# The causal masks of a four-layer transformer as bfloat16 products of 32 rows and 32 keys, in the row groups of its scores

## The chip, the core and the metric

The kernel runs on one core of a Trainium2 chip. The metric is device time in microseconds for one execution; three executions of the kernel before took 2935.04, 2935.37 and 2937.30 us, median 2935.37. A core has a matrix engine (TensorE, PE in the profile; its loads of the stationary operand are shown apart as PEld), VectorE (DVE), ScalarE (ACT), GpSimd (POOL) and SyncE (SP), which here issues all DMAs. Each engine works through its own instructions in order and waits on semaphores for the others. SBUF is the working memory of 128 partitions; TensorE writes to PSUM, which is handed out here as banks of 128 x 512 float32.

## The reference

The reference applies eight blocks in a row to x of shape (4, 512, 128) in float32, with a residual and a layer norm around each. Here the first and the third matter, and for a small part the fifth and seventh, which are attentions too.

The first block is single-head causal attention with a down-and-up projected value. The third is a transformer of four layers with eight heads of 16 features. Four of the heads look at a window of 128 keys and the 128 before it:

```python
dots = jnp.einsum('bwie,bwje->bwij', bq, bk2) * e ** (-0.5)
mask_value = -jnp.finfo(dots.dtype).max
causal_mask = tix[:, :, :, None] < kix[:, :, None, :]
pad_mask = (kix == -1)[:, :, None, :]
dots = jnp.where(causal_mask | pad_mask, mask_value, dots)
attn = jax.nn.softmax(dots, axis=-1)
```

The other four heads are causal linear attention. Each layer ends with a feed-forward part of width 512.

## The kernel before, in words

The 2048 tokens are cut into eight groups `g` of 512 tokens, each as four tiles of 128 tokens (`NT` = 4). A stage is a set of Python generators, one for each group or each piece of work; `turns` (L392) steps them by a table of start turns, and every `yield` ends a turn. What a generator emits in a turn goes to the engines in exactly that order (a manual schedule). So where an instruction stands in its engine's queue is decided by the turn in which its generator emits it, and a wait in it holds up all that its engine has behind it.

**Loads.** `program` (L1952) issues the loads through `load` (L1965), one DMA on SP for each part of a packed input (L1973). The order on SP is: `x`, small constants and the weights of the first block, the remaining constants, `l1rows`, then the weights of the four transformer layers (L2017), and then what the stages themselves ask for as they are built: after the first stage comes `l1f_quarter` and `phi` of the fourth block.

**First block, `stage_l0` (L563).** `group(g)` (L654) runs attention and feed-forward of one group; a new group starts every four turns. Beside them runs the generator `constants()` (L576): in its first steps it makes the first block's own masks (`negs`, `ident`) on ScalarE, waits eight turns (`idle(8)`, L588), and then converts the three feed-forward weights on VectorE (L590). ScalarE makes for each group the normalised input `xn` (L283), copies of projections out of PSUM (`xT` L596, `wqT`/`wkT` L667, `v` L673), the exponentials `e` (L628) and the transposed weights `eT` (L638).

**Transformer, `stage_l1_attn` (L756).** At its start VectorE and GpSimd fill some buffers (`l_val` L768, `l_max` L770, `l_ctx`), and VectorE casts the identity and the 128 x 128 causal mask to bfloat16 (L773 to L775). Then 32 mixes `l1_mix` (L832; four layers times eight groups) and 32 feed-forwards `l1_ffn` (L810) are interleaved, from the sixth mix on one in eight turns (`at`, L788). PSUM is a ring of seven banks `s`, which also serve as `mm` and `t`, and one bank `o`.

In a mix, all that is of interest is what the two sequences `b` = 0, 1 of the group do for their four local heads. A head's queries and keys lie in 32 partitions, so the four heads are the four row groups of TensorE. For each `b` four banks are taken, one for a head; four products with the identity as the stationary operand write the mask twice (two tiles of diagonal keys, 256 columns) into each bank (L886, through `mm`, L335); then the scores `kT,qT` are added to them, 32 rows each, first of 128 and then of 256 keys. VectorE takes the maxima out of the banks (`l_max`, L894) and joins two of them (L895). Later TensorE transposes the maxima (L908), `q2T` is made of them (L909), and the scores are computed a second time, transposed (`q2T,kT`), for the exponentials `e` on ScalarE (L944), which GpSimd masks (L947) and TensorE multiplies with the values (`e,l_val`). The layer norms run as statistics on VectorE (L255, L257), a power on GpSimd (`ln_rs`, L244 and L245), and normalisation on VectorE (`xn`, L264). GpSimd also adds the biases to the residual `z` (L813, L843).

**Fifth and seventh block.** `attention_pools` (L355) loads two constants, `sel` and `rows`, on SP (`att_sel`, `att_rows`) and casts `rows`, the identity and the mask to bfloat16 on VectorE (L375). Their masks stay as they are. In the seventh block, group 0 squares its rows on ScalarE into a scratch tile `last_sq` to sum them (L1673).

The functions that the change touches, and what calls them:

Of the kernel before, what the change touches and what calls it, by code (L numbers as in the profile page):

```python
# [100 lines left out]
def attention_constants():  # L101


    p = np.arange(P) % 32
    c = Pack()
    c.add("sel", ((p[:, None] < 12) & (p[:, None] % 4 == np.arange(4)[None, :])).astype(np.float32))
    c.add("rows", np.tile((p[:, None] < 12).astype(np.float32), (1, P)))
    return c


def packs(i):

    out = {"const": constants(), "att": attention_constants()}
    a = out["l0"] = Pack()
    a.add("wq", i["L0_attn_Wq"])
    a.add("wk", i["L0_attn_Wk"])
    a = out["l0v"] = Pack()
    a.add("down", i["L0_attn_Wvdown"].T)
    a.add("up", i["L0_attn_Wvup"])
    a = out["l0f"] = Pack()  # L120
    a.add("gate", i["L0_ffn_w_gate"].T)
    a.add("up", i["L0_ffn_w_up"].T)
    a.add("down", rows_to_partitions(i["L0_ffn_w_down"].T))
    r = out["l1rows"] = Pack()
    for k in range(4):
        a = out[f"l1_{k}"] = Pack()
        wq, wk, wv = (i[f"L1_attn_W{x}"][k] for x in "qkv")
        a.add("wq", heads_padded(wq[:, :64]))
        a.add("wk", heads_padded(wk[:, :64]))
        a.add("tok", np.concatenate([wq[:, 64:], wk[:, 64:], wv], axis=1))  # L130
        a.add("wo", i["L1_attn_Wo"][k])
        a.add("w1", i["L1_attn_W1"][k])
        a.add("w2", rows_to_partitions(i["L1_attn_W2"][k]))
        a.add("b1", i["L1_attn_b1"][k].reshape(4, P).T)
        for x in ("ln1_g", "ln1_b", "ln2_g", "ln2_b"):
            a.add(x, i[f"L1_attn_{x}"][k][:, None])
        r.add(f"bo{k}", i["L1_attn_bo"][k][None])
        r.add(f"b2{k}", i["L1_attn_b2"][k][None])
    a = out["l1f"] = Pack()
    a.add("phi", i["L1_ffn_phi"])  # L140

    p = np.arange(P)
    a.add("quarter", ((p[:, None] % 32 == np.arange(P)[None, :] // 32) & (p[:, None] < 96)).astype(np.float32))
    a = out["l1fb"] = Pack()
    a.add("b", i["L1_ffn_b"].reshape(16, 4, D).transpose(1, 0, 2))
    a = out["l1fw"] = Pack()
    a.add("w", i["L1_ffn_W"].transpose(1, 0, 2))
    a = out["l2"] = Pack()
    for x in "qkvo":
        a.add("w" + x, i["L2_attn_W" + x])  # L150
    a.add("w1", i["L2_ffn_w1"])
    a.add("w2", rows_to_partitions(i["L2_ffn_w2"]))
    a.add("b1", i["L2_ffn_b1"].reshape(4, P).T)
    r.add("l2b2", i["L2_ffn_b2"][None])
    a = out["l3"] = Pack()
    p = "L3_attn_"
    a.add("in", i[p + "in_proj_w"])
    for x in "BC":
        a.add(x, i[p + x + "_proj_w"].reshape(D, 16, 64)[:, SCAN_HEADS])
    a.add("out", rows_to_partitions(i[p + "out_proj_w"]))  # L160
    a.add("mfc", i[p + "m_fc_w"])
    a.add("mproj", rows_to_partitions(i[p + "m_proj_w"]))
    kw = np.repeat(i[p + "k_w"].reshape(D, 4, 1, 8), 4, axis=2).reshape(D, 128)
    a.add("qkv", np.concatenate([i[p + "q_w"], kw, i[p + "v_w"]], axis=1))
    a.add("o", i[p + "o_w"])
    a.add("afc", i[p + "a_fc_w"])
    a.add("aproj", rows_to_partitions(i[p + "a_proj_w"]))
    a.add("convw", rows_to_partitions(i[p + "conv_w"]))
    a.add("convb", i[p + "conv_b"].reshape(2, P).T)
    a.add("gain", np.repeat(i[p + "q_gain"], 8)[:, None])  # L170
    a.add("D", np.repeat(i[p + "D_param"], 16).reshape(2, P).T)
    a = out["l3rows"] = Pack()
    for x in ("resid_mix_m", "resid_mix_a"):
        a.add(x, i[p + x].reshape(1, -1))
    for x in ("mamba_scale", "m_mlp_scale", "attn_scale", "a_mlp_scale", "dt_bias", "A_log"):
        a.add(x, i[p + x][None])
    a = out["moe"] = Pack()
    a.add("gate", i["L3_ffn_gate_w"])
    for e in range(8):
        a.add(f"w1_{e}", i["L3_ffn_w1"][e])  # L180
        a.add(f"w2_{e}", rows_to_partitions(i["L3_ffn_w2"][e]))
    return out
# [17 lines left out]
class Ctx:  # L200
# [154 lines left out]
    def attention_pools(self):  # L355

        nc = self.nc
        self.vm = [self.t([P, NT, 4, D], f"at_vm{i}", 1) for i in range(2)]  # L360
        self.pieces = [self.t([P, 2, 4, 32], f"at_pc{i}", 1, dt=BF16) for i in range(2)]
        for a in self.vm + self.pieces:
            nc.gpsimd.memset(a, 0.0)
        for a in self.vm:
            for v in range(4):
                at = a[:, :, v, :].rearrange("p t (r n) -> p t r n", r=4)
                lo = 16 * (v % 2) + 8
                nc.gpsimd.memset(at[:, :, :, lo : lo + 8], 1.0)
        self.cb = {n: self.t([P, P], "b_" + n, 1, dt=BF16) for n in ("ident", "negmask", "rows")}
        self.sel = self.t([P, 4], "at_sel", 1)  # L370
        with self.tc.tile_pool(name="att", bufs=1) as pool:
            got = self.load(pool, "att")
            nc.vector.tensor_copy(self.sel, got["sel"])
            for n, a in (("ident", self.c["ident"]), ("negmask", self.c["negmask"]), ("rows", got["rows"])):
                nc.vector.tensor_copy(self.cb[n], a)  # L375

    def variants(self, src, tag):

        nc, mask = self.nc, self.c["head8"]
        out = self.t([P, 4, GT], tag, 2)  # L380
        for v in (0, 1):
            nc.scalar.activation(out[:, v, :], src, AF.Copy, scale=mask[:, v : v + 1])
        nc.gpsimd.tensor_tensor(out[:, 2:4, :], bc(src, 1, 2), bc(mask[:, 2:4], 2, GT), ALU.mult)
        return out

    def values_put(self, g, v, src):

# [175 lines left out]
def stage_l0(k, x, w, wv, wi, z, l1, y7, xT0):  # L563
# [12 lines left out]
    def constants():  # L576
        full = k.t([P, P], "negs", 1)
        gp.memset(full, NEG)
        gp.memset(negs[:, 2, :], 0.0)
        yield  # L580
        nc.scalar.copy(negs[:, 1, :], full)
        nc.scalar.copy(ident, k.c["ident"])
        ps = k.ps("s")
        k.mm(ps[:, :D], wv["down"], wv["up"])
        nc.scalar.copy(wfull, ps[:, :D])
        for t in (0, 3):
            nc.scalar.copy(negs[:, t, :], k.c["negmask"])
        yield from idle(8)  # L588
        for name in f:
            v.tensor_scalar(f[name], wi[name], float(np.float32(1.0 / 127.0)), None, ALU.mult)  # L590
            yield
# [164 lines left out]
def stage_l1_attn(k, x, ws, rows, z, then, xn, y7, xT0):  # L756
# [13 lines left out]
        nc.gpsimd.memset(a, 0.0)  # L770
    for a in k.l1_ctx:
        nc.gpsimd.tensor_copy(a[:, :, 64:68], bc(k.c["head16"], 1, 4))
    k.cb = {n: k.t([P, P], "b_" + n, 1, dt=BF16) for n in ("ident", "negmask")}  # L773
    for n, a in k.cb.items():
        nc.vector.tensor_copy(a, k.c[n])  # L775

    def ffn(i, g):
        late = i == 3 and g in k.over
# [53 lines left out]
def l1_mix(k, z, w, bo, n, hT=None):  # L832
# [1 line left out]


    nc, v = k.nc, k.nc.vector
    ident, negmask = k.cb["ident"], k.cb["negmask"]
    val, lin, ctx, mx = k.l1_val[n % 3], k.l1_lin[n % 3], k.l1_ctx[n % 2], k.l1_max[n % 2]
    heads = [slice(32 * h, 32 * h + 32) for h in range(4)]
    tiles = lambda b: [slice((2 * b + t) * P, (2 * b + t + 1) * P) for t in range(2)]  # L840
# [40 lines left out]
    for b in range(2):  # L881
        (q0, q1), both = tiles(b), slice(2 * b * P, (2 * b + 2) * P)
        ss = [k.ps("s") for _ in heads]


        for s in ss:  # L886
            k.mm(s[:, : 3 * P].rearrange("p (j n) -> p j n", j=3)[:, 0:3:2, :], ident, bc(negmask, 1, 2), True, False)
        for r, s in zip(heads, ss, strict=True):
            k.mm(s[:, 0:P], qT[r, q0], kT[r, q0], False, False)
        for r, s in zip(heads, ss, strict=True):  # L890
            k.mm(s[:, P : 3 * P], qT[r, q1], kT[r, both], False, True)
        for h, s in enumerate(ss):
            s = s[:, : 3 * P].rearrange("p (j n) -> p j n", j=3)
            v.tensor_reduce(mx[:, b, :, h, 16], s, AX.X, ALU.max, negate=True)  # L894
        v.tensor_tensor(mx[:, b, 1, :, 16], mx[:, b, 1, :, 16], mx[:, b, 2, :, 16], ALU.min)  # L895
        if b == 0:
            yield
            yield
# [729 lines left out]
def l3_gqa(k, x, xa, w, gain, mix, first):  # L1628
# [31 lines left out]
    def tail(g, yT):  # L1660
# [7 lines left out]
        if g == 0:  # L1668

            ss = k.t([P, NT], "last_ss", 1)  # L1670
            sq = k.t([P, D], "last_sq", 1)
            for t in range(NT):
                nc.scalar.activation(sq, xa[g][:, t, :], AF.Square, accum_out=ss[:, t : t + 1])  # L1673
            yield
            k.rsqrt(k.kept[0], ss, 1.0 / D, RMS_EPS)

# [275 lines left out]
def program(ctx: ExitStack, tc: tile.TileContext, xin, dram, at, out):  # L1952
# [42 lines left out]
    const.update(load(base, "const", set(at["const"]) - {"ident", "negmask"}))  # L1995
    k = Ctx(tc, const, None, None)
    k.load = load
    k.mhalf = base.tile([P, P], F32, tag="mhalf", name="mhalf")
    nc.gpsimd.memset(k.mhalf, -0.5)
    k.over = {g: base.tile([P, NT], F32, tag=f"over{g}", name=f"over{g}") for g in (NG - 2, NG - 1)}  # L2000
# [88 lines left out]
```

## Time and profile before

| what | value |
|---|---|
| median of three executions | 2935.37 us (2935.04 to 2937.30) |
| span of the profiled execution | 2932.0 us (3.4 us under that median) |
| TensorE busy (PE) | 2732.5 us, 93% |
| loads of stationary operands (PEld) | 1849.0 us, 63% |
| VectorE, ScalarE, GpSimd busy | 1951.7, 1713.0, 1017.2 us |
| mean granted TensorE clock | 0.967 |
| the first block | to about 173 us |
| the transformer | about 174 to 910 us; 21 steady periods of 22.49 us from 362 us on, then four of about 24 us |

The profile is one execution of the program on the chip. A line of a group or timeline names the source line, the engine, the operation, what it writes and reads (tile names without buffer numbers), the shape, and how often; for a matmul the shape begins with rows*columns of the array that it uses. In a timeline the first number is the start and the second the duration of the merged stretch, both in microseconds. Brackets give the idle time of the engine before the stretch and what ended it. A float32 product stands as two records, one for each pass. `b_negmask,b_ident` are the mask products. Ends of matmuls are modelled and overlap, so distances between starts say more than durations. In the chain of waits, each piece was released by the one before it.

### The profile page before, as it was taken

The numbers are of one execution on the slowest core, as the hardware profiler recorded it, in microseconds if no ns is written. First come the engines' busy times: TensorE is split into PE (matmuls) and PEld (weight loads), VectorE is DVE, ScalarE is ACT, GpSimd is POOL, SyncE is SP. The second block draws the span as 40 slices with busy tenths as digits, with TensorE's granted clock in tenths as the row PEclk, the third lists the DMA queues.
The fourth block names the chain that finished last, engine by engine and source line by source line (L and its number), as shares of the span: only waits on it lengthen the run. The fifth ranks groups of instructions, "written<-read, shape, count | busy, mean of one in ns | idle before, by whom it ended". The sixth has DMA issues, their size and how long they took to land.

```text
span 2932.0 us, 59643 instructions
## 1 busy us (share of the span) xinstructions
PE 2732.5 (93%) x23674; PEld 1849.0 (63%) x23674; DVE 1951.7 (67%) x5309; ACT 1713.0 (58%) x3568; POOL 1017.2 (35%) x1406
## 2 busy tenths in 40 slices
PE   8989999999998699999978997999999799988998
PEld 5656667766666588888843443566666444436897
DVE  5765666666676999999776774666574686737442
ACT  6746566666665577777635665444444377756443
POOL 3543333333345100000054554422231466645332
PEclk9999999999999799999989998899999899999999
DMA  4000000000000000000010000000000000010000
GB/s 105 12 1 1 2 1 2 2 2 2 5 12 27 6 14 11 10 11 9 18 62 5 1 2 1 1 1 1 1 1 1 2 1 1 1 39 21 1 16 16
DMA packets 30158, 31.30 MB, mean 11 GB/s; under 512 B 7404, under 2 KB 21292, under 8 KB 29868
## 3 DMA queue, kind: packets, MB, share of 16 engines
q1 hardware_dynamic: 29880, 27.49, 3.2%
q8 instruction: 187, 3.06, 0.4%
q14 instruction: 91, 0.75, 0.1%
HBM read 23.29 MB, written 4.19 MB: 9 GB/s over the span
## 4 chain that ended last, share of the span: by engine, by line
PE 67%; DVE 10%; ACT 9%; POOL 4%; issue 2%; DMA 0%; SPq 0%; POOLq 0%; ACTq 0%; DVEq 0%
PE ps_s L336 41%; PE ps_o L336 11%; PE ps_mm L336 7%; PE ps_s L325 3%; ACT e L944 2%; ACT at_e L491 1%; POOL ln_rs L245 1%; PE ps_t L1218 1%; DVE xn L264 1%; PE ps_xin L336 1%; PE ps_sum L336 1%; ACT L944 1%; POOL e L947 1%; DVE l_max L894 1%; ACT lg L1213 1%
## 5 line engine op out<-in xcount | busy, mean ns | idle before, releaser
L459 DVE TENSOR_REDUCE at_nm<-ps_s 128x2 f32<-128x512 f32 (+1 forms) x384 | 238.1, 681 | 118.9 <-PE ps_s L336 118.9
L491 ACT ACTIVATE at_e<-ps_s 128x512 f32<-128x512 f32 x384 | 198.1, 604 | 96.2 <-PE ps_s L336 94.0
L1502 DVE TENSOR_TENSOR scan<-ps_s,lm 128x384 f32<-128x384 f32 x256 | 124.6, 548 | 142.4 <-PE ps_s L336 142.2
L497 POOL TENSOR_SCALAR_AFFINE_SELECT at_e<-at_e 128x1024 f32<-128x1024 f32 (+1 forms) x96 | 135.1, 1407 | 209.2 <-ACT at_e L491 208.9
L245 POOL TENSOR_TENSOR ln_rs<-ln_rs,mhalf 128x4 f32<-128x4 f32 x192 | 196.3, 1022 | 15.7
L1026 POOL TENSOR_TENSOR ln_rs<-ln_mv,mendt 128x4 f32<-128x4 f32 x6 | 1.2, 198 | 510.6 <-DVE mend L1247 507.1
L244 POOL TENSOR_SCALAR ln_rs<-ln_mv 128x4 f32<-128x4 f32 x184 | 39.6, 215 | 372.9 <-DVE ln_mv L257 357.5
L894 DVE TENSOR_REDUCE l_max<-ps_s 128x3 f32<-128x384 f32 x256 | 124.8, 551 | 53.6 <-PE ps_s L336 51.2
L336 PE MATMUL ps_o<-my,meT 128*128 128x129 f32 x1024 | 142.2, 284 | 15.3 <-ACT mgot L1232 7.9
L947 POOL TENSOR_SCALAR_AFFINE_SELECT e<-e 128x512 f32<-128x512 f32 x128 | 78.9, 637 | 218.5 <-ACT e L944 218.5
L336 PE MATMUL ps_s<-qm,kT 32*128 32x512 f32 x768 | 144.3, 654 | 8.0 <-DVE at_nm L459 7.8
L336 PEld LDWEIGHTS ps_o<-my,meT 128*128 128x128 f32 x1024 | 125.8, 192 | 38.1 <-ACT meT L1220 24.4
L336 PE MATMUL ps_s<-km,qT 32*128 32x512 f32 x768 | 137.8, 664 | 11.6 <-DVE qT L1646 3.7
L336 PE MATMUL ps_mm<-mdisp,mxn 128*128 128x128 f32 x1024 | 129.5, 284 | 10.5 <-DVE mdisp L1134 10.5
L336 PEld LDWEIGHTS ps_o<-l_w,mlp_h 128*128 128x128 f32 x1024 | 126.1, 192 | 19.1 <-issue 12.8
L336 PE MATMUL ps_o<-at_e,at_vm 128*32 128x128 f32 (+1 forms) x2048 | 123.1, 337 | 15.3 <-ACT at_oT L521 15.3
L336 PE MATMUL ps_s<-mphi,mxT 128*128 128x256 f32 x448 | 123.2, 395 | 14.2 <-DVE mpart L1095 13.9
L336 PE MATMUL ps_s<-b_negmask,b_ident 128*128 128x256 bf16 (+1 forms) x640 | 125.6, 306 | 9.8 <-DVE b_negmask L775 3.1
L336 PE MATMUL ps_o<-l_w,mlp_h 128*128 128x128 f32 x1024 | 130.4, 276 | 4.0 <-ACT oT L964 3.9
L336 PEld LDWEIGHTS ps_mm<-mdisp,mxn 128*128 128x128 f32 x1024 | 124.6, 200 | 14.0 <-DVE mdisp L1134 11.9
L1479 ACT COPY BT<-ps_s 128x512 f32<-128x512 f32 x64 | 37.5, 587 | 158.1 <-PE ps_s L336 158.1
L336 PEld LDWEIGHTS <-b_ident 128*128 128x128 bf16 x656 | 57.6, 100 | 108.9 <-issue 89.1
(470 smaller groups left out, 7272.1 us busy)
## 6 DMA issues: line engine op xcount, KB each, us to landing
mw<-in_l1fw SPq DMA_DIRECT2D x16, 256.0 KB, 2.6
moe_w<-in_moe SPq DMA_DIRECT2D x16, 256.0 KB, 5.5
l_w<-in_l SPq DMA_DIRECT2D x10, 256.0 KB, 3.6
x<-in_x SPq DMA_DIRECT2D x8, 256.0 KB, 4.4
xs<-x SPq DMA_DIRECT2D x8, 256.0 KB, 2.2
out<-x SPq DMA_DIRECT2D x8, 256.0 KB, 2.3
slT<-xs SPq DMA_DIRECT2D x6, 256.0 KB, 2.7
mphi<-in_l1f SPq DMA_DIRECT2D x7, 128.0 KB, 2.0
```

The costliest lines, as they stand in the source:

```text
L244: g.tensor_scalar(out, in_, scale, eps, ALU.mult, ALU.add)
L245: g.tensor_tensor(out, out, self.mhalf[:, :n], ALU.pow)
L325: self.nc.tensor.transpose(out[:n, k * P : (k + 1) * P], src[:, k, cols], self.c["ident"])
L336: self.nc.tensor.matmul(out, lhsT=lhsT, rhs=rhs, start=start, stop=stop, skip_group_check=True)
L459: v_.tensor_reduce(nm[:, t, r, vs], s, AX.X, ALU.max, negate=True)
L491: nc.scalar.activation(e[:, r], s, AF.Exp)
L497: nc.gpsimd.affine_select(at, at, [[0, 4], [0, n], [1, P]], ALU.is_ge, 0.0, base=0, channel_multiplier=-1)
L894: v.tensor_reduce(mx[:, b, :, h, 16], s, AX.X, ALU.max, negate=True)
L944: nc.scalar.activation(e[:, h].rearrange("p j n -> p (j n)"), s[:, : 3 * P], AF.Exp)
L947: nc.gpsimd.affine_select(e[:, :, j, :], e[:, :, j, :], [[0, 4], [1, P]], ALU.is_ge, 0.0, base=0, channel_multiplier=-1)
L1479: nc.scalar.copy(s, ps)
L1502: v.tensor_tensor(m, s[:, : SEQ + P], lm[:, SCAN_HEADS[4 * (t // 2) + 2 * i + hh], :], ALU.mult)
```

## The change

- A new packed input `masks` of two parts is loaded in the first block by `constants()`: `tri` (128 x 512 float32, 256 KB) and `one` (128 x 32, 16 KB). After the eight idle turns ScalarE casts both to bfloat16 into tiles that live for the whole program (`k.tri`, `k.one`).
- The 128 x 128 mask is written in four pieces `c` of 32 keys. For each piece and each head, a 32 x 128 block of `tri` is the stationary operand, in the row group of that head, and `one` (a 32 x 32 identity, read twice) streams 64 columns. So a group of four products of 256 columns becomes sixteen products of 64 columns, each with its own load, in the order: piece 0 for the four banks, piece 1 for the four banks, and so on. The scores follow as before.
- The casts of identity and mask at the start of the transformer (L773 to L775) go.
- `rows` is loaded as one column (0.5 KB instead of 64 KB), and the cast reads it as a broadcast.
- The squares of group 0 in the seventh block are written into the tile `y`, which is free by then, instead of `last_sq`.

```diff
-    c.add("rows", np.tile((p[:, None] < 12).astype(np.float32), (1, P)))
+    c.add("rows", (p[:, None] < 12).astype(np.float32))
...
+def mask_constants():
+    p = np.arange(P)
+    c = Pack()
+    behind = 32 * np.arange(4)[None, :, None] + (p % 32)[:, None, None] > p[None, None, :]
+    c.add("tri", np.where(behind, NEG, 0.0).astype(np.float32))
+    c.add("one", (p[:, None] % 32 == np.arange(32)[None, :]).astype(np.float32))
+    return c
...
-            for n, a in (("ident", self.c["ident"]), ("negmask", self.c["negmask"]), ("rows", got["rows"])):
+            for n, a in (("ident", self.c["ident"]), ("negmask", self.c["negmask"]), ("rows", got["rows"].to_broadcast([P, P]))):
...
+    def masked(self, banks):
+        tri = self.tri.rearrange("p (c q) -> p c q", c=4)
+        for c in range(4):
+            for r, s in enumerate(banks):
+                k = slice(32 * r, 32 * r + 32)
+                self.mm(s[:, :, 32 * c : 32 * c + 32], tri[k, c, :], bc(self.one[k], 1, s.shape[1]), c == 0, False)
...
             nc.scalar.copy(negs[:, t, :], k.c["negmask"])
+        got = k.load(k.work, "masks")
         yield from idle(8)
+        for to, name in ((k.tri, "tri"), (k.one, "one")):
+            nc.scalar.copy(to, got[name])
         for name in f:
...
-    k.cb = {n: k.t([P, P], "b_" + n, 1, dt=BF16) for n in ("ident", "negmask")}
-    for n, a in k.cb.items():
-        nc.vector.tensor_copy(a, k.c[n])
...
-        for s in ss:
-            k.mm(s[:, : 3 * P].rearrange("p (j n) -> p j n", j=3)[:, 0:3:2, :], ident, bc(negmask, 1, 2), True, False)
+        k.masked([s[:, : 3 * P].rearrange("p (j n) -> p j n", j=3)[:, 0:3:2, :] for s in ss])
...
-            sq = k.t([P, D], "last_sq", 1)
             for t in range(NT):
-                nc.scalar.activation(sq, xa[g][:, t, :], AF.Square, accum_out=ss[:, t : t + 1])
+                nc.scalar.activation(y[:, t, :], xa[g][:, t, :], AF.Square, accum_out=ss[:, t : t + 1])
...
+    k.tri, k.one = (base.tile([P, at["masks"][n][1]], BF16, tag="mask_" + n, name="mask_" + n) for n in ("tri", "one"))
```

More of the change, by code (lines that the diff above doesn't have):

```diff
@@ L106, in attention_constants @@
     c.add("sel", ((p[:, None] < 12) & (p[:, None] % 4 == np.arange(4)[None, :])).astype(np.float32))
-    c.add("rows", np.tile((p[:, None] < 12).astype(np.float32), (1, P)))
+    c.add("rows", (p[:, None] < 12).astype(np.float32))
[6 more added lines that the diff above has]
+    c.add("one", (p[:, None] % 32 == np.arange(32)[None, :]).astype(np.float32))
     return c
 def packs(i):
-    out = {"const": constants(), "att": attention_constants()}
+    out = {"const": constants(), "att": attention_constants(), "masks": mask_constants()}
     a = out["l0"] = Pack()
@@ L836, in l1_mix @@
     nc, v = k.nc, k.nc.vector
-    ident, negmask = k.cb["ident"], k.cb["negmask"]
     val, lin, ctx, mx = k.l1_val[n % 3], k.l1_lin[n % 3], k.l1_ctx[n % 2], k.l1_max[n % 2]
```

## The prediction

> **What bounds the kernel now.** I read the page's span and chain first, then the chain of waits and the timeline of one steady period of the four-layer transformer (where the masks are), then the timeline of ScalarE and of the SP queue at the start of the run (where the new load and its casts fall).
>
> The page: its span, its chain by engine, and the group of all mask products.
>
> ```profile
> span 2932.0 us, 59643 instructions
> PE 67%; DVE 10%; ACT 9%; POOL 4%; issue 2%; DMA 0%; SPq 0%; POOLq 0%; ACTq 0%; DVEq 0%
> L336 PE MATMUL ps_s<-b_negmask,b_ident 128*128 128x256 bf16 (+1 forms) x640 | 125.6, 306 | 9.8 <-DVE b_negmask L775 3.1
> ```
>
> Two thirds of the chain is TensorE. Of the 640 mask products 256 (64 groups of four) are the transformer's; the rest belong to two other attentions and stay.
>
> The timeline of ScalarE, then of the SP queue, in the first stage (start, duration), and the time to landing of the DMAs issued from 37 to 42 us.
>
> ```profile
> 24.62 0.58 ACT L638 COPY eT<-ps_s 128x512 f32<-128x512 f32 x1 [0.95 <-PE ps_s L636]
> 26.98 0.58 ACT L673 COPY v<-ps_s 128x512 f32<-128x512 f32 x1 [1.77 <-PE ps_s L336]
> 27.46 1.65 ACT L283 ACTIVATE xn<-x,ln_nb,ln_rs 128x128 f32<-128x128 f32 x4
> ```
> ```profile
> 41.25 0.43 SPq L1973 DMA_DIRECT2D l1f_quarter<-in_l1f  x1
> 41.72 0.43 SPq L2030 DMA_DIRECT2D phi<-in_l1f  x1
> ```
> ```profile
> l_w<-in_l SPq DMA_DIRECT2D x2, 256.0 KB, 3.3
> phi<-in_l1f SPq DMA_DIRECT2D x1, 128.0 KB, 2.3
> l1f_quarter<-in_l1f SPq DMA_DIRECT2D x1, 64.0 KB, 1.9
> ```
>
> The queue issues one load each 0.47 us, and the loads behind the transformer's weights go out only at 41.25 us. By then ScalarE has long passed 25 us.
>
> The windows: span, then busy time of PE, PEld, DVE, ACT, POOL. The first follows the `v` copy above; the second is one steady period.
>
> ```profile
> 26.98:60.00 33.02, 31.64 (x158) 18.85 (x157) 23.53 (x121) 25.75 (x64) 12.78 (x24) 1.00 0.32 75
> 433.88:456.37 22.49, 22.25 (x220) 15.70 (x219) 14.23 (x52) 14.28 (x31) 7.84 (x11) 1.00 0.01 2
> ```
>
> Both are dense on TensorE, so time lost in the first stage is not made good from slack, and the steady period looks as if any saving on TensorE would count. The next views say it does not. The chain of waits of a steady period where its first mask group (A) stands, then VectorE, GpSimd and TensorE up to the transposes of the maxima:
>
> ```profile
> 474.88 0.79 ACT e L944 x2
> 475.66 0.04 issue
> 475.70 1.14 PE ps_s L336 x17
> ```
> ```profile
> 476.86 1.95 DVE L894 TENSOR_REDUCE l_max<-ps_s 128x3 f32<-128x384 f32 x4 [1.27 <-PE ps_s L336]
> 478.93 0.86 DVE L255 BATCH_NORM_STATS2 ln_st<-z 128x6 f32<-128x128 f32 x4
> 482.17 0.54 DVE L895 TENSOR_TENSOR l_max<-l_max 128x4 f32<-128x4 f32 x1
> ```
> ```profile
> 481.41 1.27 POOL L813 TENSOR_TENSOR z<-z,l1rows 128x512 f32<-128x512 f32 x1
> ```
> ```profile
> 478.70 0.60 PE L336 MATMUL ps_s<-b_negmask,b_ident 128*128 128x256 bf16 x4
> 479.23 0.94 PE L336 MATMUL ps_s<-kT,qT 32*128 32x128 f32 x16
> 482.32 0.78 PE L908 MATMUL ps_s<-const_ident,l_max 128*128 128x128 f32 x4
> ```
>
> The last mask of group A waits until 475.70 for a bank that an exponential frees. From the scores behind it VectorE works without a gap (maxima, L895, statistics, aggregates, to 480.07), which releases GpSimd's `ln_rs` and then its sum L813 (to 482.69). L895 of group B, 0.17 us long elsewhere, lasts 0.54 and ends at 482.71, right after L813; the fourth transpose of the maxima waits for it. Group B (478.70) lies inside that path, not on it.
>
> **The change part by part.** The sum is made against the profiled execution (span 2932.0); the median of the three runs is 2935.4, so 3.4 us lie around the span, and I keep them.
>
> *The load of the masks and its casts (first stage): the large term.* The generator issues the load at its second step, but SP works in order, and the built SP order has `masks_tri` (256 KB) and `masks_one` (16 KB) right behind the last transformer weight, where `l1f_quarter` is now: issue 41.25 and 41.72. Landing: quarter and phi together, 192 KB, are in by 41.72 + 2.3 = 44.0; 64 KB more at the pace at which phi followed quarter (128 KB in 0.85 us) gives 44.4. The two casts stand on ScalarE between the `eT` copy, which ends at 25.2, and the `v` copy. So ScalarE stands still from 25.2 to 44.4 us. Then 0.5 us for the 128x512 cast (the like copies start 0.48 apart) and 0.2 for the small one: `v` starts at about 45.2, not 26.98: +18.2. With the 256 KB load at 2.6 us (the sixteen `mw` loads) or 3.9 (the slowest `l_w` from 30 us on) it is 17.5 to 18.9. Queued behind: every later ScalarE instruction; TensorE first misses the `xn` of 27.46 (its transposes at 29.04), and after it VectorE and GpSimd. Given back: what waited for VectorE is ready by then (ScalarE idled 0.69 us before `e` at 31.25): -0.7, from 0 to -1.5. Added: TensorE is idle for 17 us. After the idle stretch that ends at 134.76 its clock was granted at 0.55 until 137.0 and 0.78 from there to 140; about 3.6 us at half speed is 1.8 us of work, some of it beside ScalarE: +1.2, from 0 to 2.5. Sum for this stage **+18.7**, bounds +16.0 and +21.4. The loads behind move by 0.95 us and are wanted hundreds of us later: nothing.
>
> *The masks, 256 products of 256 columns to 1024 of 64.* Now: a group's products start 0.109 us apart ((0.60 - 0.273)/3); from its first to the scores' first load is 0.53, of which 0.09 is the pause that TensorE shows at each switch of row groups. After it, the pause comes ahead of the masks and none behind. What a 32-row bfloat16 product costs is not in a mask row; the nearest row is the one of four 32-row bfloat16 products:
>
> ```profile
> 1568.20 0.39 PE L336 MATMUL ps_s<-at_mT,b_rows 32*128 32x512 bf16 x4
> ```
>
> Alone each lasts 0.374, so four groups start within 0.02: 7 ns apart, side by side. A product of 64 columns streams 0.027 (256 take 0.107). A round of four so costs 0.027 (7 ns each) to 0.054 (load and stream in turn); the far bound is 0.107, the step of the 128-column float32 scores. A group: 0.09 + 0.2 = about 0.28 instead of 0.53, a quarter of a microsecond less, 16 us over 64 groups if all of it counted.
>
> It does not. Steady periods (21 of 22.49 us): group A's last bank comes at 475.70 whatever TensorE does; from there to the scores is 0.20 now, and three rounds, 0.08 to 0.16, afterwards: 0.07 saved. Group B's saving ends in the wait for L895, which moves with group A alone. 21 x 0.07 = **-1.5**, from -2.4 to +2.7 (rounds of 0.107).
>
> [...] The row shows 7 ns between row groups, so I go by the row.
>
> The first eight mixes, with long waits on other engines and TensorE at clock 0.50 (178 to 187 us): groups take up to 1.0 us there; half of 16 groups x 0.25: **-2.0**, from 0 to -6. The last four periods (24.05 us, no bank wait): 4 x 0.18 = **-0.7**, from 0 to -1.5.
>
> *The two casts of L775 gone.* 0.2 us on VectorE at 176.2, counted in the -2.0: TensorE's 3.1 us wait for them gives nothing more, as kT is ready only at 174.9 and VectorE is late anyway with statistics, `qm` and maxima.
>
> *`rows` as one column.* The DMA of 64 KB becomes 0.5 KB. VectorE waited 0.37 us for it at 1518.2, once: **-0.3** (0 to -0.4); the second is not waited for. *Squares into `y`*: four activations of 0.31, same engine and size: 0, hidden by the 2.4 us that ScalarE waits ahead of them; without that cover a write wait, under 0.1.
>
> Sum: +18.7 - 1.5 - 2.0 - 0.7 - 0.3 = **+14.2**, 2935.4 + 14.2 = 2949.6.
>
> **The rivals.**
> 1. *TensorE's saving counts in full.* For it: TensorE is busy 22.25 of 22.49 us. Against: the wait of the fourth transpose for L895. It would give 18.7 - 16 - 0.3 = +2.4, 2938.
> 2. *The stall is absorbed* (the other side): the landing comes before ScalarE needs it, or the casts cost nothing because the stage has 18 us to spare. For it: only that ScalarE is busy 25.75 of 33.02 us. Against: issue at 41.25, and TensorE at 31.64 of 33.02. It gives -4.5, 2930.9; it decides if `masks_tri` lands before about 27 us.
> 3. *Both at once*: -16.3, 2919.
> [...]
>
> **How the numbers follow.** Forecast 0.80; rival 1 0.08, rival 2 0.03, rival 3 0.03, rival 4 0.06. The forecast's bounds add to +5.7 (16.0 - 2.4 - 6 - 1.5 - 0.4) and +24.1, ends that need every term at its edge; I take 2940 to 2957, which leaves out rivals 2 and 3, half of 1 and half of 4. A measurement tells 0.2% (5.9 us) from no change: slower (above 2941.3) 0.89, within 0.2% 0.07, faster 0.04.
>
> **What the profile after would show.** ScalarE idle from 25.2 to about 44.4 us in front of the cast of `mask_tri`, released by a DMA; the first stage longer by 16 to 21 us (`l_val` memsets at about 192.5, not 173.9); mask groups of sixteen that take 0.1 to 0.25 us, without a pause before the scores; the steady period between 22.35 and 22.49 us; TensorE waiting longer ahead of L908. The prediction is wrong if the casts are released early, or if the period falls to about 22.0.

## The result, and the profile after

The changed kernel takes 2944.7 us (median of five, 2942.39 to 2952.05), the kernel before 2935.04 us beside it: ratio 1.0036 with a 95% interval of 1.0025 to 1.0047, so 7 to 14 us slower. The profiled execution has a span of 2940.7 us, 8.7 more than that of before.

The page of the kernel after, its span and its chain by engine:

```profile
span 2940.7 us, 61176 instructions
PE 65%; DVE 15%; ACT 11%; POOL 5%; issue 2%; SPq 1%; DMA 1%; POOLq 0%; ACTq 0%; DVEq 0%
```

VectorE's share of the chain has grown from 10 to 15%; where it came in is seen below. First the loss. The timeline of ScalarE of the kernel after in the first stage (start, duration, in brackets the idle time ahead and what ended it), then the SP queue and the time to landing:

```profile
25.88 0.58 ACT L662 COPY eT<-ps_s 128x512 f32<-128x512 f32 x1 [1.20 <-PE ps_s L660]
42.67 0.62 ACT L612 CAST mask_tri<-masks_tri 128x512 bf16<-128x512 f32 x1 [16.21 <-DMA masks_tri<-in_masks]
43.20 0.21 ACT L612 CAST mask_one<-masks_one 128x32 bf16<-128x32 f32 x1
43.32 0.58 ACT L697 COPY v<-ps_s 128x512 f32<-128x512 f32 x1
```
```profile
39.91 0.43 SPq L1991 DMA_DIRECT2D masks_tri<-in_masks  x1
```
```profile
masks_tri<-in_masks SPq DMA_DIRECT2D x1, 256.0 KB, 2.7
```

ScalarE stands still for 16.21 us until the DMA lands, and the `v` copy comes at 43.32 instead of 26.98. The windows after the `v` copy and of one steady period answer to those shown of before (span, busy time of PE, PEld, DVE, ACT, POOL, granted clock):

```profile
43.32:76.34 33.02, 31.15 (x143) 17.84 (x144) 16.36 (x75) 25.48 (x64) 7.09 (x13) 0.92 0.01 2
462.37:484.75 22.38, 21.72 (x243) 15.28 (x243) 14.35 (x51) 14.29 (x31) 7.84 (x11) 1.00 0.00 1
```

TensorE is 0.53 us less busy in a steady period (22.25 before), but the period is only 0.11 shorter. If each instruction is set against the same one of before, its delay is +16.6 us at 60 us; +15.1 at the end of the first stage (`l_val` memsets at 189.0, before 173.9); +9.5 when the steady periods begin; +6.9 at 900 us. After that only code that is nearly the same follows, and yet there are steps of +1.7 (at 922), -3.0 (at 1520 to 1565), +4.5 (2610 to 2640) and -1.5 (2725 to 2900), to +8.5 at the end. The runs below separate most of these pieces.

### The profile page after: what moved, and what is told of

Its sections match the earlier page's. It is cut to its first block, busy times and chain, and to the rows that moved or that the text cites. A ratio compares the mean times of both kernels' runs of the same rounds, so it can differ in the third digit from the quotient of the medians.

```text
span 2940.7 us, 61176 instructions
## 1 busy us (share of the span) xinstructions
PE 2717.4 (92%) x24442; PEld 1834.2 (62%) x24442; DVE 1953.8 (66%) x5307; ACT 1712.8 (58%) x3570; POOL 1018.4 (35%) x1406
## 4 chain that ended last, share of the span: by engine, by line
PE 65%; DVE 15%; ACT 11%; POOL 5%; issue 2%; SPq 1%; DMA 1%; POOLq 0%; ACTq 0%; DVEq 0%
PE ps_s L347 40%; PE ps_o L347 10%; PE ps_mm L347 7%; DVE l_max L913 3%; PE ps_s L336 2%; ACT e L963 2%; POOL ln_rs L256 1%; ACT at_e L512 1%; DVE ln_st L266 1%; DVE xn L275 1%; PE ps_t L1237 1%; PE ps_xin L347 1%; POOL e L966 1%; PE ps_sum L347 1%; ACT L963 1%
## 5 line engine op out<-in xcount | busy, mean ns | idle before, releaser
L347 PE MATMUL ps_s<-xT,l_w 128*128 128x512 f32 x256 | 126.1, 613 | 2.5 <-ACT xT L827 1.3
L275 DVE TENSOR_SCALAR xn<-z,ln_mv,ln_rs 128x128 f32<-128x128 f32 x252 | 74.9, 361 | 70.1 <-POOL ln_rs L256 70.1
```

The costliest lines, as they stand in the source:

```text
L275: self.nc.vector.tensor_scalar(out[:, k, :], src[:, k, :], mv[:, k, 0:1], rs[:, k : k + 1], ALU.subtract, ALU.mult)
L347: self.nc.tensor.matmul(out, lhsT=lhsT, rhs=rhs, start=start, stop=stop, skip_group_check=True)
```

## The experiments

All ratios are against the kernel before on the same chip, with their 95% interval.

### Only the load and its casts

The kernel before with the change's load and casts, where the change has them; its own masks are used as before, and the cast ones by nobody.

```diff
             nc.scalar.copy(negs[:, t, :], k.c["negmask"])
+        got = k.load(k.work, "masks")
         yield from idle(8)
+        for to, name in ((k.tri, "tri"), (k.one, "one")):
+            nc.scalar.copy(to, got[name])
```

> The kernel before with the change's load and casts, at the same places, and nothing else of it; all masks are written as before and the cast masks are not used. Theory: +15.1 to +16.6 us from the first stage, 2950 to 2952 us (ratio 1.0050 to 1.0058), and no other step in the trace beyond what two executions differ by; the transformer's periods stay at 22.49 us. The change stands at +9.7, so the masks' own saving would be 5.5 to 7. Rival (the late stages' steps of +1.7, -3.0 and +4.5 us in the change's trace belong to the load or the first stage's shift): they appear here too, with the same signs and places. Rival (absorbed): 2935.

Measured: 2950.45 us, ratio 1.0048 (1.0035 to 1.0061), 10 to 18 us slower. ScalarE waits 15.81 us for `masks_tri` and casts at 42.55; the delay is +16.6 us at 60 us and +15.1 at the end of the stage, as in the change; the steady periods stay at 22.49. So the load and its casts are the loss, and in the traces the rest of the change is a gain of 5.4 us by 900 us (+12.3 here, +6.9 with the change). Of the change's late steps, that at 922 us and that of +4.5 at 2610 to 2640 us do not appear here, and 1520 to 1565 us brings +3.3 instead of -3.0: the load does not make them.

It also shows that the profile of before is not a clean yardstick. With unchanged masks, this kernel gains 1.6 us at 225 to 260 us and 1.4 at 335 to 362 us. The windows of these stretches, first of the kernel before, then of this one (the third number from the right is the granted TensorE clock):

```profile
225.00:260.00 35.00, 32.73 (x298) 22.77 (x297) 19.61 (x60) 21.27 (x49) 10.74 (x15) 0.95 0.00 1
335.00:362.00 27.00, 25.48 (x239) 17.75 (x238) 15.22 (x57) 14.61 (x34) 8.78 (x12) 0.94 0.00 1
```
```profile
225.00:260.00 35.00, 32.63 (x325) 21.36 (x325) 26.13 (x88) 20.19 (x48) 13.07 (x19) 1.00 0.00 1
335.00:362.00 27.00, 25.16 (x264) 17.89 (x263) 18.25 (x63) 14.71 (x33) 7.85 (x11) 1.00 0.01 2
```

In the profiled execution of before, TensorE's clock was granted at half speed for a moment in each of them (0.50 from 230.49 to 233.90 and from 339.72 to 343.13 us); here it was not. The drop from +16.6 to +15.1 at about 135 us, in both kernels with the stall, lies where before had a clock of 0.61 (134 to 138 us); at its counterpart in the changed kernel (150 to 154 us) it is 1.00. This one is no accident of one profile: each of the ten executions without the stall has such a stretch between 112 and 159 us, and neither of the two with the stall has. The other two come and go: the kernel before with GpSimd's sum moved (below) has the first and not the second, the one with late casts the second and not the first.

### Late casts, and an early load

Two ways to take the wait away and keep the masks. The first moves the casts nine turns back:

```diff
-        for to, name in ((k.tri, "tri"), (k.one, "one")):
-            nc.scalar.copy(to, got[name])
         for name in f:
             v.tensor_scalar(f[name], wi[name], float(np.float32(1.0 / 127.0)), None, ALU.mult)
             yield
+        yield from idle(6)
+        for to, name in ((k.tri, "tri"), (k.one, "one")):
+            nc.scalar.copy(to, got[name])
```

> Only the place of the two mask casts on ScalarE differs from the change: they are emitted nine turns later, long after the masks have landed (42.7 us). Theory (the first stage's stall is the whole loss): ScalarE no longer stands still from 26.5 us on, the l_val memsets come at 174 to 175 us (before 173.9, after 189.0), and the time falls by 15.1 to 16.6 us against the change: 2928 to 2930 us, about 6 us under the kernel before (ratio 0.997 to 0.999). Rival (the stage absorbs the stall, or the loss lies in the later stages): the memsets come earlier but the time stays at 2942 to 2946. Second rival (the casts themselves cost ScalarE): 0.7 us are kept, not told apart here.

The second leaves the casts and issues the load ahead of the transformer's rows and weights:

```diff
+    k.masks = load(p0, "masks")
     rows1 = load_rows(base, "l1rows")
...
-        got = k.load(k.work, "masks")
+        got = k.masks
```

> The casts stand where the change has them, but the masks are loaded ahead of the transformer's rows and weights, issued at about 17.8 us instead of 39.91. Theory (what ScalarE waits for is the place of the load in SP's queue): landing at 20.5 to 22 us, before ScalarE comes to the casts at 26.5, no stall, and the same time as with late casts, 2928 to 2931 us; the casts then cost 0.7 us on ScalarE at most. Rival (the casts at that place are what costs, by their order on ScalarE ahead of the v copy): most of the stall stays, 2940 us or more.

Measured: 2927.86 us, ratio 0.9974 (0.9963 to 0.9984), and 2928.4 us, 0.9975 (0.9966 to 0.9983): both 5 to 11 us faster than before. The `l_val` memsets come at 173.7 us with late casts, where they were before. With the early load, issued at 17.24, ScalarE of that kernel goes straight from the `eT` copy into the casts, and then still waits for TensorE ahead of the `v` copy, which hides them:

```profile
28.02 0.58 ACT L662 COPY eT<-ps_s 128x512 f32<-128x512 f32 x1 [0.95 <-PE ps_s L660]
28.50 0.62 ACT L612 CAST mask_tri<-masks_tri 128x512 bf16<-128x512 f32 x1
29.02 0.22 ACT L612 CAST mask_one<-masks_one 128x32 bf16<-128x32 f32 x1
30.38 0.58 ACT L697 COPY v<-ps_s 128x512 f32<-128x512 f32 x1 [1.14 <-PE ps_s L347]
```

So neither the place of the casts on ScalarE nor the casts themselves cost anything measurable; the lateness of the load at that place does. This execution is 3.4 us late by 28 us, not because of the early load: the first run of the moved sum below, whose load is not early, is 3.7 us late there too. What makes them late is not shown.

### New masks in one group alone

Late casts, and the new products only for one of the two sequences, the old ones for the other; the casts of identity and mask on VectorE are back.

```diff
-        k.masked([s[:, : 3 * P].rearrange("p (j n) -> p j n", j=3)[:, 0:3:2, :] for s in ss])
+        if b == 0:
+            k.masked([s[:, : 3 * P].rearrange("p (j n) -> p j n", j=3)[:, 0:3:2, :] for s in ss])
+        else:
+            for s in ss:
+                k.mm(s[:, : 3 * P].rearrange("p (j n) -> p j n", j=3)[:, 0:3:2, :], k.cb["ident"], bc(k.cb["negmask"], 1, 2), True, False)
```

The other kernel has `b == 1` in the condition.

> Late casts; the new mask products only for the first sequence (group A), the old four products of 256 columns for the second (group B), with the casts of identity and mask on VectorE back. Theory (group A is on the period's path, group B's saving ends in the wait for VectorE): the steady periods fall as with all new masks, by 0.11 us each (stretch from 400 to 800 us shorter by 1.9 to 2.0), and the transformer as a whole keeps at least 3 of the 7 us. Rival (every group's TensorE time counts): half, 0.05 to 0.06 us a period, 1.0 in that stretch.

> Late casts; the new mask products only for the second sequence (group B). Theory: the steady periods stay at those of before, within 0.02 us (0 to 0.3 in the stretch from 400 to 800 us), although group B's masks take 0.13 instead of 0.53 us, and TensorE's fourth transpose of the maxima waits longer for VectorE's join; some of the first eight mixes may gain. Rival (every group's TensorE time counts): 0.05 to 0.06 us a period, as for group A. If both kernels gain and their sum is that of all new masks, the rival stands.

Measured: 2931.93 us, ratio 0.9992 (0.9983 to 1.0000), and 2931.98 us, 0.9992 (0.9983 to 1.0001). The times can't tell them apart; the traces can, one execution each (distances between VectorE's joins of group A's maxima; of the first six distances the sum):

| masks | first six mixes, us | steady period, us | last periods, us | group B's join, us |
|---|---|---|---|---|
| old in both (load and casts alone) | 135.26 | 22.49 | 24.04 | 0.53 |
| new in A | 134.42 | 22.37 | 23.91 | 0.49 |
| new in B | 133.38 | 22.49 | 24.03 | 0.76 |
| new in both (late casts) | 132.72 | 22.375 | 23.92 | 0.77 |

In the steady periods the whole gain of 0.115 us is group A's; group B's products give nothing, and the join after them lasts 0.23 us longer. In the first six mixes, where no join is held (0.17 us each), group B gives 1.9 us and A 0.8 by the table; but the first of these distances varies by itself (15.34 to 16.01 us in seven executions with all new masks). In the other five B gives 0.9 us, A 0.5 and both together 1.3. The rival of equal shares falls.

### What holds group B

The join L895 (L914 in the changed kernel) ends right after GpSimd's bias sum in every steady period. The first try emitted that sum one turn later:

```diff
-    k.nc.gpsimd.tensor_tensor(z, z, bc(b2, 1, NT), ALU.add)
     yield
     h = k.t([P, 4, GT], "mlp_h", 2)
...
+        if f == 1:
+            k.nc.gpsimd.tensor_tensor(z, z, bc(b2, 1, NT), ALU.add)
         if f % 2:
             yield
```

> Late casts as in the run of that name, and GpSimd's sum of the bias into z in the feed-forward is emitted one turn later, so that it no longer lies beside VectorE's join of the maxima. Theory (group B's saving ends in the wait for that join, which lasts until GpSimd's sum ends, 0.54 to 1.09 us instead of 0.17): the join falls to about 0.17 us, TensorE's fourth transpose of the maxima comes 0.3 to 0.6 us earlier, and a period falls from 22.38 to between 21.8 and 22.2 us: 5 to 15 us under the run with late casts alone. Rival (another wait takes its place, the bank that an exponential frees or VectorE's own work): the join shortens, the period stays within 0.1 us of 22.38, and the time within 3 us of the run with late casts. Second rival (the sum at its new place delays GpSimd's masking of e or ln_rs, or holds another operation of VectorE): slower by some us.

Measured: 2929.56 us, ratio 0.9980 (0.9969 to 0.9990), steady period 22.38, join 0.76. The edit moved nothing: GpSimd has no other instruction in that turn, so the sum still followed `ln_rs` at once. Nothing follows from it but that a later place in the code is not a later time. The second try puts it behind GpSimd's next two instructions, `l_ctx` and the mix's bias sum, with the new masks and late casts, and alone in the kernel before:

```diff
     ps = k.ps("o").rearrange("p (t d) -> p t d", t=NT)
+    k.nc.gpsimd.tensor_tensor(z, z, bc(b2, 1, NT), ALU.add)
     w2 = w["w2"].rearrange("p (c n) -> p c n", c=4)
```

> Late casts, and GpSimd's sum of the feed-forward's bias is emitted two turns later, behind the product for l_ctx and the mix's own bias sum in GpSimd's queue (one turn later, in the run before, moved nothing: GpSimd had nothing in between and started it at the same place). Theory (VectorE's join of group B is held until that sum ends): the join falls from 0.77 to 0.17 us in every period, the 0.26 us that TensorE waits ahead of the fourth transpose go, a period falls by 0.2 to 0.35 us, and the time by 5 to 10 us against late casts alone: 2918 to 2923 us. Rival (VectorE's own chain or a bank takes over): the join shortens, the period stays within 0.05 us. Rival (the join's length is its own, whatever GpSimd does): it stays at 0.77 us.

> The kernel before with the same move of GpSimd's sum and nothing else. If group B's saving only waits behind the held join, this gains less than the same move does with the new masks, by up to 0.2 us a period. If VectorE's own work between the two groups' maxima (join of A, statistics, maxima of B) hides group B's masks anyway, both gain the same: what the old join loses, 0.54 minus 0.17 us less what TensorE is late by itself, 0 to 0.2 us a period, 0 to 6 us in all (2929 to 2937).

Measured: with the new masks 2921.49 us, ratio 0.9955 (0.9943 to 0.9967); alone 2930.9 us, 0.9989 (0.9979 to 0.9998). All joins fall to 0.17 us, in the kernel before too. With the new masks the period falls by 0.475 us against late casts, more than the 0.2 to 0.35 expected, and 0.3 us more than the same move gives alone (expected: up to 0.2 more). The steady periods make a table of two by two:

| steady period, us | sum where it was | sum two turns later |
|---|---|---|
| old masks | 22.49 | 22.32 |
| new masks | 22.375 | 21.90 |

With the join held the masks save 0.115 us a period, without it 0.42. So group B's saving was there and ended in the wait for the held join: that rival (VectorE's own chain hides it) falls. The chain of waits over one period from group A's last bank to the transposes of the maxima shows how, first of the kernel before, then of the change, then of the change with late casts and the later sum (start, duration, engine, tile, line):

```profile
453.21 1.14 PE ps_s L336 x17
454.35 1.44 PE ps_o L336 x32
455.78 0.59 PE ps_s L325 x4
456.37 3.62 PE ps_s L336 x40
459.99 0.61 PE ps_s L908 x4
```
```profile
462.37 1.06 PE ps_s L347 x29
463.43 1.95 DVE l_max L913 x4
465.39 0.17 DVE l_max L914
465.56 0.78 DVE ln_st L266 x4
466.34 0.28 DVE ln_mv L268 x4
466.62 1.85 DVE l_max L913 x4
468.49 0.77 DVE l_max L914
469.31 0.33 PE ps_s L927
```
```profile
467.99 1.01 PE ps_s L347 x29
469.00 1.49 PE ps_o L347 x32
470.48 0.58 PE ps_s L336 x4
471.07 3.28 PE ps_s L347 x52
474.35 0.44 PE ps_s L928 x4
```

Before, the stretch is 7.39 us (453.21 to 460.60), and the profile's chain puts all of it on TensorE, group B's masks in the 3.62 us. Yet the last transpose waits for the held join there too. The four transposes have one group in the profile; these lines of the three kernels show their loads of the stationary operand in 20 mixes and, behind the second bar, the idle time before them and what ended it. In the first line the join is L895, in the second L914; the third, whose join is L915, names only the maxima (L914 there):

```profile
L908 PEld LDWEIGHTS ps_s<-const_ident,l_max 128*128 128x128 f32 x80 | 10.7, 141 | 15.4 <-issue 5.8 <-DVE l_max L894 5.1 <-DVE l_max L895 4.5
L927 PEld LDWEIGHTS ps_s<-const_ident,l_max 128*128 128x128 f32 x81 | 10.7, 140 | 21.5 <-DVE l_max L914 10.4 <-issue 5.8 <-DVE l_max L913 5.3
L928 PEld LDWEIGHTS ps_s<-const_ident,l_max 128*128 128x128 f32 x80 | 10.1, 141 | 10.9 <-issue 5.8 <-DVE l_max L914 5.1
```

By the starts of the transposes, which follow each other in 0.109 us when nothing holds them, the last one is 0.12 us late in each steady period before, 0.42 us after the change, 0.08 with the new masks in A alone, 0.46 with them in B alone, and not at all with the later sum; wherever it is late it starts 0.06 us behind the end of the join. So before the change the held join was already the later of two ways, by 0.12 us, and all that group B's masks gave went into this wait. After the change the wait is long enough for the profile to lead the chain over VectorE, 7.27 us, of which VectorE has 5.8; over 20 mixes that is most of its larger share on the page. With the sum out of the way TensorE leads, 6.80 us. The difference of 0.60 to before is 0.13 in A's piece, 0.34 in the piece with group B's masks, 0.17 in the transposes that no longer wait, less 0.04 elsewhere. The rest of the period, 15.1 us, is the same in all three.

### The sum in the last layer

With the later sum the last periods are 24.22 us, 0.30 longer than with late casts alone (23.92): VectorE waits 3.38 us for an `ln_rs` behind the sum. The last run puts it one turn later still in the last layer, beside a second run of the kernel above.

```diff
-    k.nc.gpsimd.tensor_tensor(z, z, bc(b2, 1, NT), ALU.add)
+    if not last:
+        k.nc.gpsimd.tensor_tensor(z, z, bc(b2, 1, NT), ALU.add)
     w2 = w["w2"].rearrange("p (c n) -> p c n", c=4)
     for t in range(NT):
+        if last and t == 1:
+            k.nc.gpsimd.tensor_tensor(z, z, bc(b2, 1, NT), ALU.add)
```

> As the run with GpSimd's sum moved by two turns, but in the last layer it is emitted one turn later still, behind the masking of e and the ln_rs that VectorE there waits for (3.38 us of idle time ahead of xn in a last period, 0.2 to 0.3 us a period longer than with the old place). Theory: each of the last four periods falls from 24.22 to between 23.0 and 23.7 us, the steady periods of 21.90 stay, and the time falls by 2 to 5 us against the earlier place, to 2917 to 2920 us. Rival (the sum then makes the second ln_rs or the sum of z late): no gain or a loss of up to 2 us.

> The same kernel as the run with the sum moved by two turns, beside the next variant on the same chip: 2919 to 2923 us, steady periods of 21.90 and last ones of 24.22 us. Its trace shows which of the late steps (at about 920, 1520, 1840, 1880, 2610 and 2730 us) differ between two executions of one kernel: if they come from the half-speed stretches of TensorE's clock, they come and go here too, by about 1.5 us each, with the granted clock in those windows; if they belong to a kernel, they stay.

Measured: 2922.69 us, ratio 0.9965 (0.9953 to 0.9977), against 2916.85 us, 0.9945 (0.9930 to 0.9959) for the earlier place. The theory missed: the last periods are 23.93, not 23.0 to 23.7, and at the change of place one period is 0.94 us longer, which uses up that gain. The second run of the kernel above took less than the 2919 to 2923 us expected of it. Of the 5.3 us between the two profiles 2.1 lie before 30 us, where the kernels do not differ yet, 0.3 in the transformer's periods and 2.7 between 880 and 930 us, where it ends; whether these 2.7 come from the moved sum or from the clock was not separated. The later sum at one place, with late casts, remains the fastest kernel of this study, 13 and 17 us under the kernel before in its two runs.

Which late steps stay? Set against before, the two executions of the fastest kernel differ at 922 us (none, +1.6), 1840 and 1880 us (none, -1.5 each): these come and go. The step at 2610 to 2640 us stays (+4.5 and +4.6), with a granted clock of 0.77 over the 45 us around it, against 0.92 before. All nine executions of kernels that hold the change's `rows` and squares have it (+4.5 to +4.6; +2.2 with late casts alone), and neither of the two that hold only other parts or none of the change (the load and casts alone, the kernel before with the sum moved). By the end of the program 3.1 to 3.3 us of it are left in eight of the nine, 0.1 with late casts alone. So it goes with the change.

## Why the prediction was right

The forecast of a slower kernel held, for the reason given: the load is late for ScalarE, and the masks' saving on TensorE hardly reaches the period.

- **The load and its casts**, forecast +18.7, bounds +16.0 to +21.4. Measured +16.6 up to 60 us and +15.1 at the stage's end, 1.5 of the difference being a half-speed stretch that the kernels without the stall have (at 134 us before) and those with it have not; the forecast has no such term. The mis-sized term is the landing: 42.67 us, not 44.4. SP issued the load at 39.91, not 41.25 (between 39.72 and 41.84 in the executions seen with this order), and it took 2.8 us, not 3.15. The half-speed clock after the stall is there (0.50 from 42 to 48 us), and with what VectorE gives back it adds 0.3 us to the delay; forecast were +1.2 and -0.7.
- **The products.** A free group has its sixteen starts within 0.107 us, 7 ns apart on average, and the first score starts 0.127 us behind its first start (0.53 before): 32 ns a round of four, between the forecast's 27 and 54 ns, without a pause ahead of the scores. The 27 is the author's estimate, a quarter of 0.107 us for 256 columns; the trace of before has 0.109 from start to start. Rival 4, to which the prediction gives 0.06, is that the small products are slow, in rounds of 0.107 us or more: no run shows it, and it falls.
- **Steady periods**, forecast -0.07 us each, -1.5 in all. Measured -0.115 each, -2.2 in the 19 steady distances that the trace of before has (not 21). Most of it is the term that was forecast: from the start of A's last mask product to the first score it is 0.10 us instead of 0.20. That group B gives nothing is right and shown, and "lies inside that path, not on it" holds, with a margin of only 0.12 us: so much the last transpose already waited for the held join.
- **The first eight mixes**, forecast -2.0 (0 to -6). Against the profile of before it is -5.6; against the kernel that has the stall but the old masks it is -2.8. The rest was the two clock steps in the profile of before.
- **The last four periods**, forecast -0.7. Measured -0.11 each, -0.4; the forecast took the masks' 0.18 us as a saving there, but the join is held for 1.09 us in both kernels.
- **`rows` and the squares**, forecast -0.3 and 0. VectorE no longer waits for `att_rows`, but it does not with the load and casts alone either, where `rows` is unchanged, and the steps around it (-3.0 us here, +3.3 there) are larger than the 0.37 us in question: not told apart. The squares were not nothing: into `last_sq` the four start 0.43 us apart, into the four parts of `y` 0.30, and the kernel is 0.4 us earlier behind them; no run shows the case without cover, for which the prediction names a write wait of under 0.1 us. Some 200 us later comes the step of +4.5 us, +3.1 in the end, a loss for which the forecast has no term. No run separates the squares from the rest of the change there, so its cause stays open.

With late steps left out the pieces add up to +15.1 - 2.8 - 2.2 - 0.4 = +9.7; measured is 1.0036 of 2935, +10.6 (7 to 14), which also holds the seventh block's +3.1 and whatever the clock does. The forecast of +14.2 was too high in the first stage by 3.6 us and lacked these 3.1: its closeness is in part luck, its direction is not. The 3.4 us that it keeps around the span are 1.7 to 1.8 in all executions with both numbers on record; the rest lay between executions. The rival that all of TensorE's saving counts would have needed a steady period of 22.0 us; that came only with GpSimd's sum moved.

## What to carry to other kernels

A cast put in an in-order queue waits for its DMA with everything behind it (here for 16.21 us): find the load's place in the issuing queue, work out its landing, and put the consumer behind that; here nine turns turned +0.36% into -0.26%. When work is taken off the busiest engine, look for a second path that ends as late before counting the saving, and look at what holds it; here moving one instruction of another engine took 0.475 us off a steady period, where the new masks had taken 0.115. Before reading a small step between two profiles as an effect, compare the granted clock in that stretch, or profile a kernel in which only the suspect differs; a step that every execution of one kernel and none of the other shows is an effect, even if it is one of the clock.

## What was not expected of the hardware

**Half-speed stretches of TensorE that come and go between executions of one kernel.** The same six products of the fastest kernel in its two runs. First the windows from their start to their end (span, busy times, and the granted clock third from the right), then the timeline of TensorE; the first fence of each pair is the first run:

```profile
1856.70:1861.50 4.80, 4.78 (x7) 2.12 (x8) 4.55 (x7) 1.63 (x3) 1.34 (x1) 0.57 0.01 2
```
```profile
1854.90:1857.60 2.70, 2.70 (x7) 1.26 (x8) 2.52 (x5) 1.38 (x2) 0.57 (x1) 1.00 0.01 3
```
```profile
1856.72 3.78 PE L347 MATMUL ps_s<-nT,l_w 128*128 128x512 f32 x4 [0.67 <-ACT nT L1367]
1860.29 1.29 PE L347 MATMUL ps_s<-nT,l_in 128*128 128x512 f32 x2
```
```profile
1854.88 1.99 PE L347 MATMUL ps_s<-nT,l_w 128*128 128x512 f32 x4 [0.68 <-ACT nT L1367]
1856.70 1.02 PE L347 MATMUL ps_s<-nT,l_in 128*128 128x512 f32 x2
```

The first four take 3.78 us in one execution and 1.99 in the other, behind the same wait; the clock over the six is 0.57 and 1.00. Steps of this kind cost about 1.5 us each, and the spread of whole executions goes with the mean granted clock: in 25 executions of the kernel before, those with a mean clock of 0.968 or more took 2929.8 to 2933.7 us, those with 0.964 or less 2935.9 to 2941.0. In the 29 of another session it goes less strictly: those with 0.968 or more took 2929.1 to 2938.0 us. In the clock records of before and of the change all half-speed stretches of one record begin whole multiples of 3.413 us apart (of before at 134.92, 175.88 and 230.49 us: 12 and 28 times 3.413 behind the first), and all but the one that the end of the program cuts off last 3.41 us or a multiple of it (of before 6.83, 10.24, 13.65 and more). What sets this grid, and what makes a stretch begin, is not shown. Where the changed kernel has its step at 1520 to 1565 us, before had a clock of 0.50 from 1524.14 to 1527.55 and from 1537.80 to 1541.20 us, and the change 1.00 from 1523 to 1560; that the step is of this kind is likely and was not shown.

**VectorE's small join lasts until GpSimd's sum ends.** An operation on 128x4 elements, 0.17 us long when alone, lasts 0.49 to 1.09 us where it starts beside GpSimd's sum of 128x512, and ends right behind it (at 482.71 us, the sum at 482.69); moving only the sum gave 0.17 back in every steady period of the kernel before. What of the sum holds the join is not shown.
